# A corner table of two pixels a row, and the first chunk transposed by TensorE

## The chip, the cores and the metric

The kernel runs on one core of one Trainium2 chip. The metric is the device time of one execution in microseconds (us), as the median of the runs shown. The engines are named as in the profile: PE (TensorE, matrix products; PEld its weight loads), DVE (VectorE), ACT (ScalarE), POOL (GpSimd) and SP (SyncE). SP, ACT and POOL also issue DMAs; their queues are written SPq, ACTq and POOLq.

## The reference

The input `x` has 4 images of 128 channels and 64 x 64 pixels, in float32. Two layers are computed.

Layer 0 is `x + deform_conv(group_norm(x))`. A 3 x 3 convolution of the normalized image gives, for each output pixel and each of 9 taps, an offset in y and x and a mask. Every tap is sampled bilinearly at its shifted place, with zero outside the image, and the samples are multiplied with the weights:

```python
v00 = gather(y0i, x0i); v01 = gather(y0i, x1i)
v10 = gather(y1i, x0i); v11 = gather(y1i, x1i)
samples = v00*(1-wy)*(1-wx) + v01*(1-wy)*wx + v10*wy*(1-wx) + v11*wy*wx
out = jnp.einsum('bckhw,ock->bohw', samples * mask, w_flat) + bias
```

Layer 1 treats the 4096 pixels of an image as tokens of 128 features. It adds an attention block (16 heads of 8 dimensions, queries, keys and values all being one cosine feature map of the tokens, softmax over all 4096 keys, then a small feed-forward) and a layer of 8 experts of which the best two are mixed.

## The kernel before

An image is worked on in 8 chunks of 512 pixels. `prepare(b)` makes an image ready for attention, the main loop runs attention, and `finish` takes a finished chunk through the rest of layer 1. `prepare` and `finish` are generators that say before each piece what it needs of PE and DVE. A planner (`Beside`), which keeps its own clock from estimated costs, places their pieces beside the attention steps while the program is built. The result is a fixed order of instructions on every engine; each engine works through its own in order. Before the first chunk of image 0 is ready, only `prepare(0)` runs.

**`prepare(b)`** loads the image into `xc` (L766), normalizes it (L456), and builds a *corner table* in DRAM (`corner_table`). Before, a row of the table holds four pixels, the corners of one bilinear cell, 4 x 128 floats or 2 KB; there are 67 x 67 rows (`TW` = 67), two tables, used in turn. Each chunk of 1024 pixels is transposed by PE to tokens (`tok_ps`, L464), copied by DVE to `tok` (L467), and written to the table by DMAs (L476). Every pixel is a corner of four cells, so it is written four times: 8 DMAs of 256 KB for 1024 pixels (two row parities by four corners), each in pieces of 512 bytes, 32 DMAs an image. For image 0 they are shared evenly between SP and ACT, for the others all are on SP. `tok` shares its 3 buffers (tag `v`) with the gathered samples, so the fourth chunk waits until the first has been written. The rim of the table is zeroed by `borders` (L304, L305): for table 0 on ACT at the start, for table 1 on SP when image 1 begins. The constants are loaded on ACT after the borders.

**`offsets`** multiplies the image with the offset weights (`om_ps`, L507) in two halves, turns the result (`oc_ps`, L519) and computes on DVE the table index `idx` (L551) and the four bilinear weights `wt` (L557, L559), which include the mask `mk`. For the mask ACT computes an exponential (L529).

**`deform`** goes through the image in 96 units. A unit is 128 pixels and 3 taps. POOL gathers for each tap 128 table rows with one indirect DMA (L575), two units ahead of their use. DVE multiplies with the weights (L589) and adds the four corners (L591, L592). The samples then stand with pixels on partitions and the convolution needs channels there. So DVE transposes 32 x 32 blocks (L599, three a unit); after four units the result `tr` goes to a DRAM buffer `smd` in 4 DMAs on SP (L612) and comes back in 4 DMAs as `sT` with the blocks in place (L643). Twelve units, three such trips, make a chunk.

**`convolved`** multiplies `sT` with the 9 weight taps (`conv_ps`, issued through a helper, L273), adds bias and the input `xr` (L666), turns the result (`x_ps`, L673), and goes on to `features`: layer norm, the cosine features, and their parking in DRAM as `kTd`, `qTd` and `fqd`. Attention loads keys (`kT`, L1133), values (`qf`, L1135) and queries (`qT`, L1143) on SP from there.

**Attention** computes scores `sc` (L1155), exponentials on ACT (L1164) and sums `acc` (L1172). For image 0 it starts on the first chunk while the others are still prepared. Partial sums of such runs are parked in DRAM (`part`, L1031), loaded again as `cu` (L1344) and added (L1376); a run that needs no earlier sum is copied (L1374). In the later images exponentials are also reused transposed: parked as `etd` (L1056) and loaded as `et` (L1090, used at L1108), again on SP. All these loads and stores stand on SP in one order with the table writes.

Of the kernel before, what the change touches and what calls it, by code (L numbers as in the profile page):

```python
# [30 lines left out]
KK = 9  # L31
# [165 lines left out]
def need(pe=0.0, dve=0.0, lat=0.0, hold=False, after=0.0):  # L197

    return pe, dve, lat, hold, after
# [11 lines left out]
def tr(n):  # L213

    return 0.13 + 0.115 * n
# [3 lines left out]
def kernel(  # L219
# [74 lines left out]


    NTAB = 2
    tabs = [dram.tile([TW * TW, 4 * C], F32, name=f"tab{i}") for i in range(NTAB)]
    def borders(tab, queue):
        zero = work.tile([P, 4, 4, P], F32, tag="st", name="zero", bufs=NST)
        zero = zero.rearrange("p r h x -> p r (h x)")[:TW, :2]  # L300
        nc.gpsimd.memset(zero, 0.0)
        tv = tab.rearrange("(y x) c -> y x c", x=TW)
        for s in (0, TW - 2):
            queue.dma_start(out=tv[s : s + 2].rearrange("y x c -> x y c"), in_=zero)  # L304
            queue.dma_start(out=tv[2 : TW - 2, s : s + 2, :], in_=zero[: TW - 4])  # L305
# [143 lines left out]
    def corner_table(b, xc, mg, rs, tab):  # L449


        tv = tab.rearrange("(y x) (k c) -> y x k c", x=TW, c=C)
        for ch in range(NBLK // 8):
            yield need(dve=ve(1024), lat=0.3)
            part = xc[:, 1024 * ch : 1024 * (ch + 1)]
            nc.vector.tensor_scalar(part, part, mg, rs, ALU.subtract, ALU.mult)  # L456
            tok = work.tile([P, 3, 4 * C], F32, tag="v", name=f"tok{b}_{ch}", bufs=NV)
            tok = tok.rearrange("p k (q c) -> p (k q) c", c=C)[:, :8]
            for i in range(0, 8, 4):
                yield need(pe=tr(4), dve=ve(512), lat=FREE)  # L460
                pt = misc(f"tok_ps{b}_{ch}_{i}")
                for n in range(4):
                    j = 8 * ch + i + n
                    nc.tensor.transpose(  # L464
                        pt[:, C * n : C * (n + 1)], xc[:, P * j : P * (j + 1)], ident
                    )
                nc.vector.tensor_copy(  # L467
                    tok[:, i : i + 4, :], pt.rearrange("p (i c) -> p i c", c=C)
                )
            def put(ch=ch, tok=tok):  # L470
                for par in range(2):
                    for k in range(4):
                        y0 = 16 * ch + par + 2 - k // 2
                        x0 = 2 - k % 2
                        queue = nc.scalar if b == 0 and k % 2 else nc.sync
                        queue.dma_start(  # L476
                            out=tv[y0 : y0 + 15 : 2, x0 : x0 + WW, k].rearrange("y x c -> x y c"),
                            in_=tok[WW * par : WW * (par + 1)],
                        )

            beside.later(beside.dve, put)

    def offsets(b, xn, idx, wt):
# [3 lines left out]
        for half in range(2):  # L487
# [55 lines left out]
            def of_axis(t, a):  # L543
                return t.rearrange("p j (k a) -> p j k a", a=2)[:, :, :, a]
# [10 lines left out]
            for dy in range(2):  # L555
                yield need(dve=ve(144, 3), lat=0.2)
                nc.vector.tensor_tensor(ix, of_axis(p if dy else up, 0), mk, ALU.mult)  # L557
                for dx in range(2):
                    nc.vector.tensor_tensor(  # L559
                        wt[:, blk, :, 2 * dy + dx], ix, of_axis(p if dx else up, 1), ALU.mult  # L560
                    )

    def deform(b, tab, idx, wt):
# [19 lines left out]
        for n, (ch, kg, j) in enumerate(units):  # L583
            progress[b] = 0.1 + 0.9 * n / len(units)
            v, landed = ahead.pop(0)
            v4 = v.rearrange("p k (q c) -> p (k q) c", c=C)
            w12 = wt[:, j, 3 * kg : 3 * kg + 3, :].rearrange("p k q -> p (k q)")
            yield need(dve=ve(1536), after=landed)
            nc.vector.tensor_tensor(v4, v4, w12[:, :, None].to_broadcast([P, 12, C]), ALU.mult)  # L589
            yield need(dve=ve(768) + ve(384))  # L590
            nc.vector.tensor_tensor(v[:, :, : 2 * C], v[:, :, : 2 * C], v[:, :, 2 * C :], ALU.add)  # L591
            nc.vector.tensor_tensor(v[:, :, :C], v[:, :, :C], v[:, :, C : 2 * C], ALU.add)  # L592

            yield need(dve=ve(384))
            if j % 4 == 0:
                beside.flush(sent)
                tr9 = work.tile([P, 4, 4, 4, 32], F32, tag="st", name=f"tr{b}_{ch}_{kg}", bufs=NST)
            for k in range(3):
                nc.vector.transpose(  # L599
                    out=tr9[:, k, :, j % 4, :],  # L600
                    in_=v[:, k, :C].rearrange("p (c i) -> p c i", i=32),
                )
            if n + AHEAD < len(units):
                beside.later(beside.dve, lambda u=units[n + AHEAD]: ahead.append(gather(*u)))
            if j % 4 < 3:
                continue
            while kg == 0 and len(featuring) > 1:
                yield need(lat=1.0)

            def put(ch=ch, kg=kg, tr9=tr9):  # L610
                for o in range(4):
                    nc.sync.dma_start(  # L612
                        out=smd[ch % 2][:, 3 * kg : 3 * kg + 3, :, o].rearrange(
                            "i k c n -> i (k c) n"
                        ),
                        in_=tr9[32 * o : 32 * (o + 1), :3].rearrange("p k c j t -> p (k c) (j t)"),
                    )
# [12 lines left out]
        while featuring:  # L630
            yield need(lat=1.0)

    def convolved(b, ch):

        xr = work.tile([P, CH], F32, tag="p2", name=f"xr{b}_{ch}", bufs=NP2)
        nc.sync.dma_start(out=xr, in_=xf[b, :, CH * ch : CH * (ch + 1)])
        yield need(lat=2.5)

        sT = big.tile([P, KK, CH], F32, tag="xs", name=f"sT{b}_{ch}")

        def get(kg):
            for c in range(4):
# [2 lines left out]
                    in_=smd[ch % 2][:, 3 * kg : 3 * kg + 3, c].rearrange("i k o n -> i k (o n)"),  # L645
                )

        get(0)
        yield need(lat=6.0)
        get(1)  # L650
        yield need(lat=4.0)
        for k in range(KK):
            if k == 2:
                get(2)
            for hf in range(2):
                last = k == KK - 1 and hf == 1
# [6 lines left out]
                )  # L663
        for o in range(4):
            of_block = xr.rearrange("p (j o t) -> p j o t", o=4, t=32)[:, :, o]
            nc.vector.scalar_tensor_tensor(  # L666
                of_block, po[:, P * o : P * (o + 1)].rearrange("p (j t) -> p j t", t=32), bconv_sb,
                of_block, ALU.add, ALU.add,
            )
# [786 lines left out]
```

## Time and profile before

| | |
|---|---|
| median of 3 runs | 7870.18 us (7869.32 to 7878.19) |
| the profiled execution | 7908.98 us, span 7907.1 us |
| PE busy | 7194.3 us, 91% of the span |
| ACT busy | 6874.6 us, 87% |
| DVE busy | 4487.9 us, 57% |
| POOL busy | 1644.6 us, 21% |
| chain that ended last | PE 78%, DMA 8%, DVE 3%, SPq 3% |
| gathers (L575) | 1152, mean 1254 ns on POOL |
| table writes (L476) | 112 on SP, 16 on ACT |

The page gives one execution. Its span runs from the first to the last instruction; 1.9 us lie around it. Busy shares are averages over stages that have different limits, so the stages have to be looked at one by one: the page cuts the span in 40 slices, and the trace can be asked for the busy time of any stretch, for the instructions in order of time, and for what ended each engine's idle time.

### The profile page before, as it was taken

Reading aid. Unit: us, or ns where it says so; the run is one execution under the profiler, and the core shown is the slowest. Engines: PE = TensorE matmul, PEld = TensorE weight load, DVE = VectorE, ACT = ScalarE, POOL = GpSimd, SP = SyncE. Lnnn points to the kernel's source line nnn. Section 1 sums busy time; section 2 is a strip of 40 time slices with the busy share of each in tenths; the row PEclk is TensorE's granted clock in tenths of the full one; section 3 lists DMA queues with packets and bytes.
Section 4 is the critical chain, followed back from the end, with each engine's and each line's share of the span. In section 5 each row is a group of like instructions: output and inputs, shape, how many; then the busy total and the mean of one; then the engine's idle time right before and its main releaser. Section 6 shows DMA issues by size and latency. Waiting matters only on the chain.

```text
span 7907.1 us, 182019 instructions
## 1 busy us (share of the span) xinstructions
PE 7194.3 (91%) x73664; PEld 2524.1 (32%) x73664; DVE 4487.9 (57%) x9024; ACT 6874.6 (87%) x7441; POOL 1644.6 (21%) x1326
## 2 busy tenths in 40 slices
PE   2378979999998999999999989989999999999997
PEld 1122222333333333333333333333333333333333
DVE  5666436666453667777554567766444554445434
ACT  0267978988998988989999988888999999999995
POOL 4544114343100332332000133432000000000000
PEclk6688988999999999999999999999999999999998
DMA  6776558888666878898666788988655577877762
GB/s 180 215 214 208 158 150 251 272 260 269 194 190 181 254 228 254 261 293 266 189 187 180 211 278 270 286 282 276 188 175 168 157 234 238 256 240 247 241 212 81
DMA packets 968439, 1757.98 MB, mean 222 GB/s; under 512 B 170864, under 2 KB 436088, under 8 KB 916908
## 3 DMA queue, kind: packets, MB, share of 16 engines
q1 hardware_dynamic: 862590, 1436.61, 60.1%
q0 software_dynamic: 92160, 302.06, 11.9%
q8 instruction: 578, 9.47, 0.5%
q10 hardware_dynamic: 12846, 7.67, 0.4%
q14 instruction: 265, 2.17, 0.1%
HBM read 1063.83 MB, written 682.13 MB: 221 GB/s over the span
## 4 chain that ended last, share of the span: by engine, by line
PE 78%; DMA 8%; DVE 3%; SPq 3%; issue 3%; ACT 3%; POOL 1%; another core or an unknown queue 0%; ACTq 0%; DVEq 0%; POOLq 0%
PE acc L1172 38%; PE sc L1155 23%; PE acc L1108 5%; PE e_ps L273 3%; PE conv_ps L273 3%; ACT e L1164 3%; PE f_ps L273 2%; DMA sT<-smd 2%; DMA et<-etd 1%; DMA kT<-kTd 1%; DMA etd<-st 1%; SPq L476 1%; PE om_ps L507 1%; DMA v<-tab,idx 1%; DVE v L589 1%
## 5 line engine op out<-in xcount | busy, mean ns | idle before, releaser
L1164 ACT ACTIVATE e<-sc 128x1024 f32<-128x1024 f32 x7400 | 6871.5, 1065 | 863.7 <-PE sc L1155 584.6
L1172 PE MATMUL acc<-e,qf 128*32 128x512 f32 x29600 | 3982.3, 608 | 46.1 <-DVE cu L1376 32.9
L1155 PE MATMUL sc<-qT,kT 32*128 32x512 f32 x14800 | 2404.0, 502 | 317.8 <-ACT e L1164 148.2
L1155 PEld LDWEIGHTS sc<-qT,kT 32*128 32x128 f32 x14800 | 960.2, 184 | 3745.1 <-ACT e L1164 3089.6
L575 POOL DMA_INDIRECT v<-tab,idx x1152 | 1444.7, 1254 | 1880.2 <-DVE tr L599 1158.3
L1046 DVE STREAM_TRANSPOSE st<-e 128x1024 f32<-128x1024 f32 x792 | 937.8, 1222 | 833.1 <-ACT e L1164 640.7
L1172 PEld LDWEIGHTS acc<-e,qf 128*32 128x32 f32 x29600 | 804.0, 110 | 614.4 <-issue 339.8
L375 POOL TENSOR_TENSOR r<-ln_t,expo 128x4 f32<-128x4 f32 x96 | 112.3, 1170 | 3151.2 <-DVE ln_t L373 3113.4
L589 DVE TENSOR_TENSOR v<-v,wt 128x1536 f32<-128x1536 f32 x384 | 665.9, 1734 | 103.6 <-DMA v<-tab,idx 78.5
L1108 PE MATMUL acc<-et,qf 128*32 128x128 f32 x12672 | 528.7, 283 | 55.5 <-DMA et<-etd 47.5
L273 PE MATMUL conv_ps<-sT,wconv_sb 128*32 128x256 f32 x4608 | 380.7, 407 | 125.0 <-DMA sT<-smd 121.9
L970 DVE TENSOR_TENSOR eo<-e_ps,gt 128x512 f32<-128x512 f32 x256 | 175.0, 685 | 548.7 <-PE e_ps L273 538.3
L1108 PEld LDWEIGHTS acc<-et,qf 128*32 128x32 f32 x12672 | 305.7, 110 | 259.3 <-issue 191.9
L591 DVE TENSOR_TENSOR v<-v 128x768 f32<-128x768 f32 x384 | 367.3, 957 | 10.7
L1374 DVE COPY cu<-acc 128x512 f32<-128x512 f32 x128 | 88.5, 691 | 442.0 <-PE acc L1172 392.6
L599 DVE STREAM_TRANSPOSE tr<-v 128x128 f32<-128x128 f32 x1152 | 266.0, 282 | 39.0 <-DMA etd<-st 21.1
L592 DVE TENSOR_TENSOR v<-v 128x384 f32<-128x384 f32 x384 | 215.4, 561 | 13.3
L273 PEld LDWEIGHTS conv_ps<-sT,wconv_sb 128*32 128x32 f32 x4608 | 96.9, 110 | 274.6 <-issue 255.1
L375 POOL TENSOR_TENSOR rstd<-lt_t,expo 128x4 f32<-128x4 f32 x32 | 54.3, 1696 | 554.8 <-DVE lt_t L373 554.8
L273 PE MATMUL f_ps<-w_sb,h 128*32 128x128 f32 x4096 | 165.4, 281 | 0.0
L855 DVE TENSOR_SCALAR h<-h_ps,b_sb 128x512 f32<-128x512 f32 x128 | 94.8, 743 | 102.3 <-PE h_ps L853 96.0
L1376 DVE TENSOR_TENSOR cu<-cu,acc 128x512 f32<-128x512 f32 x38 | 26.1, 686 | 207.1 <-PE acc L1172 118.9
(219 smaller groups left out, 3008.8 us busy)
## 6 DMA issues: line engine op xcount, KB each, us to landing
etd<-st SPq DMA_DIRECT2D x1584, 256.0 KB
et<-etd SPq DMA_DIRECT2D x396, 1024.0 KB
kT<-kTd SPq DMA_DIRECT2D x400, 256.0 KB
smd<-tr SPq DMA_DIRECT2D x384, 192.0 KB
sT<-smd SPq DMA_DIRECT2D x384, 192.0 KB
qf<-fqd SPq DMA_DIRECT2D x400, 144.0 KB
qT<-qTd SPq DMA_DIRECT2D x166, 256.0 KB
atd<-cu SPq DMA_DIRECT2D x128, 256.0 KB
```

What stands on the lines that cost most here:

```text
L273: nc.tensor.matmul(dst[c : c + 32], lhsT=lhsT[:, c : c + 32], rhs=rhs, start=start, stop=stop)
L575: nc.gpsimd.indirect_dma_start(out=v[:, k, :], out_offset=None, in_=tab, in_offset=bass.IndirectOffsetOnAxis(ap=idx[:, j, kk : kk + 1], ax ...
L589: nc.vector.tensor_tensor(v4, v4, w12[:, :, None].to_broadcast([P, 12, C]), ALU.mult)
L591: nc.vector.tensor_tensor(v[:, :, : 2 * C], v[:, :, : 2 * C], v[:, :, 2 * C :], ALU.add)
L592: nc.vector.tensor_tensor(v[:, :, :C], v[:, :, :C], v[:, :, C : 2 * C], ALU.add)
L599: nc.vector.transpose(out=tr9[:, k, :, j % 4, :], in_=v[:, k, :C].rearrange("p (c i) -> p c i", i=32),)
L970: nc.vector.tensor_tensor(ws[hf], pe.rearrange("p (e c) -> p e c", c=C), gt[:, i, 4 * hf : 4 * (hf + 1), None].to_broadcast([P, 4, C]), AL ...
L1046: nc.vector.transpose(out=st[:, :, 2 * pr : 2 * pr + 2, :].rearrange("p o h (q j) -> p o (h q) j", j=32), in_=es[pr].rearrange("p h (q o i ...
L1108: nc.tensor.matmul(acc[32 * h : 32 * (h + 1), P * kt : P * (kt + 1)], lhsT=qf[:, t, QW * h : QW * h + 32], rhs=e[:, :, h, 32 * t : 32 * (t ...
L1155: nc.tensor.matmul(ps[i // 2][:, i % 2, :], lhsT=kT[h : h + 32, P * (t % 4) : P * (t % 4 + 1)], rhs=qT[h : h + 32, :], start=True, stop=True,)
L1164: nc.scalar.activation(e, ps[pr], AF.Exp, scale=1.0 / math.sqrt(HD))
L1172: nc.tensor.matmul(acc[32 * h : 32 * (h + 1), :], lhsT=qf[:, t % 4, QW * h : QW * h + 32], rhs=es[h // 2][:, h % 2, :], start=(t == ts[0]) ...
```

## The change

A table row now holds two pixels, the upper and the lower corner at one x, 2 x 128 floats or 1 KB. A gather still takes 2 KB from the row of its index, which is that row and the next, the corners at x + 1. One more row at the end of the table, zeroed by its own small DMA, keeps the last gather inside. A pixel is written twice instead of four times: 16 DMAs an image. For image 0 the row parity chooses the queue, ACT writing the odd rows of the first three chunks and SP all others, including both parities of the fourth. The borders keep their number of DMAs and halve their bytes. The weights `wt` change their order with the corners.

For the first chunk of image 0 the three tap blocks of a unit are transposed by PE into a PSUM bank and copied by DVE into `sT_first`; the trip through `smd` is left out. The pixels of that chunk stand in their natural order, so `convolved` takes `in_order` and loads nothing but `xr`. All other chunks go through `smd` as before. The planner is told of the new needs, and so it also places pieces of the first image's later chunks differently: for instance PE's convolution of the second chunk now begins in the fourth attention run and not in the second. From the end of that stretch on, PE's instructions stand in the same order as before.

```diff
-    tabs = [dram.tile([TW * TW, 4 * C], F32, name=f"tab{i}") for i in range(NTAB)]
+    tabs = [dram.tile([TW * TW + 1, 2 * C], F32, name=f"tab{i}") for i in range(NTAB)]
     def borders(tab, queue):
         zero = work.tile([P, 4, 4, P], F32, tag="st", name="zero", bufs=NST)
-        zero = zero.rearrange("p r h x -> p r (h x)")[:TW, :2]
+        zero = zero.rearrange("p r h x -> p r (h x)")[:TW, :2, : 2 * C]
         nc.gpsimd.memset(zero, 0.0)
-        tv = tab.rearrange("(y x) c -> y x c", x=TW)
+        tv = tab[: TW * TW].rearrange("(y x) c -> y x c", x=TW)
+        queue.dma_start(out=tab[TW * TW :], in_=zero[:1, 0])
...
             def put(ch=ch, tok=tok):
                 for par in range(2):
-                    for k in range(4):
-                        y0 = 16 * ch + par + 2 - k // 2
-                        x0 = 2 - k % 2
-                        queue = nc.scalar if b == 0 and k % 2 else nc.sync
+                    for k in range(2):
+                        y0 = 16 * ch + par + 2 - k
+                        queue = nc.scalar if b == 0 and par == 1 and ch < 3 else nc.sync
                         queue.dma_start(
-                            out=tv[y0 : y0 + 15 : 2, x0 : x0 + WW, k].rearrange("y x c -> x y c"),
+                            out=tv[y0 : y0 + 15 : 2, 2 : 2 + WW, k].rearrange("y x c -> x y c"),
                             in_=tok[WW * par : WW * (par + 1)],
                         )
...
-                        wt[:, blk, :, 2 * dy + dx], ix, of_axis(p if dx else up, 1), ALU.mult
+                        wt[:, blk, :, 2 * dx + dy], ix, of_axis(p if dx else up, 1), ALU.mult
...
+            if (b, ch) == (0, 0):
+
+                if (kg, j) == (0, 0):
+                    sT = big.tile([P, KK, CH], F32, tag="xs", name="sT_first")
+                yield need(pe=tr(3), dve=ve(384))
+                pt = misc(f"sT_ps{j}_{kg}")
+                for k in range(3):
+                    nc.tensor.transpose(pt[:, P * k : P * (k + 1)], v[:, k, :C], ident)
+                nc.vector.tensor_copy(
+                    sT[:, 3 * kg : 3 * kg + 3, P * j : P * (j + 1)],
+                    pt[:, : 3 * P].rearrange("p (k c) -> p k c", c=P),
+                )
+                if n + AHEAD < len(units):
+                    beside.later(beside.dve, lambda u=units[n + AHEAD]: ahead.append(gather(*u)))
+                if (kg, j) == (2, 3):
+                    featuring.append(True)
+                    beside.add("prepare", convolved(b, ch, sT), 0.5, True)
+                continue
...
-    def convolved(b, ch):
+    def convolved(b, ch, sT=None):
...
+        in_order = sT is not None
+        if not in_order:
+            yield need(lat=2.5)
+
+            sT = big.tile([P, KK, CH], F32, tag="xs", name=f"sT{b}_{ch}")
...
+        if not in_order:
+            get(0)
+            yield need(lat=6.0)
+            get(1)
+            yield need(lat=4.0)
         for k in range(KK):
-            if k == 2:
+            if k == 2 and not in_order:
                 get(2)
...
+            if in_order:
+                of_block = xr[:, P * o : P * (o + 1)].rearrange("p (j t) -> p j t", t=32)
```

More of the change, by code (lines that the diff above doesn't have):

```diff
@@ L449, in corner_table @@
     def corner_table(b, xc, mg, rs, tab):
-        tv = tab.rearrange("(y x) (k c) -> y x k c", x=TW, c=C)
+        tv = tab[: TW * TW].rearrange("(y x) (k c) -> y x k c", x=TW, c=C)
         for ch in range(NBLK // 8):
@@ L631, in deform @@
             yield need(lat=1.0)
-    def convolved(b, ch):
+    def convolved(b, ch, sT=None):
         xr = work.tile([P, CH], F32, tag="p2", name=f"xr{b}_{ch}", bufs=NP2)
         nc.sync.dma_start(out=xr, in_=xf[b, :, CH * ch : CH * (ch + 1)])
-        yield need(lat=2.5)
-        sT = big.tile([P, KK, CH], F32, tag="xs", name=f"sT{b}_{ch}")
+        in_order = sT is not None
+        if not in_order:
+            yield need(lat=2.5)
+            sT = big.tile([P, KK, CH], F32, tag="xs", name=f"sT{b}_{ch}")
         def get(kg):
@@ L646, in get @@
                 )
[L648 to L651, printed above, removed]
+        if not in_order:
[3 more added lines that the diff above has]
+            yield need(lat=4.0)
         for k in range(KK):
-            if k == 2:
+            if k == 2 and not in_order:
                 get(2)
```

## The prediction

> **What bounds the kernel now.** Part 2 of the page, slice by slice, says that TensorE (PE) is full from about 800 us on, and nearly idle before 250. So I read three stretches where PE waits: the start, the change of image near 1000 us, and two short ones later. First the busy time by stage (columns: stretch, length, then PE, weight loads, DVE, ACT, POOL, granted clock, DMA share, GB/s), then the instructions in order of time (start, duration, engine or queue, line; in brackets the idle time before it and what ended it).
>
> ```profile
> 50.00:100.00 50.00, 12.56 (x152) 6.95 (x152) 23.20 (x61) 1.95 (x3) 8.98 (x9) 0.60 0.72 178
> 100.00:150.00 50.00, 0.00 (x0) 0.00 (x0) 40.32 (x62) 0.00 (x0) 39.20 (x27) 0.50 0.59 168
> 200.00:250.00 50.00, 4.78 (x20) 2.27 (x24) 41.01 (x81) 3.79 (x5) 32.31 (x24) 0.50 0.66 208
> ```
>
> ```profile
> 13.00 9.00 ACTq L305 DMA_DIRECT2D tab<-zero  x1
> 34.23 10.28 PE L507 MATMUL om_ps<-xc,wom_sb 128*32 128x256 f32 x144 [5.01 <-DMA wom_sb<-in_wom_dram]
> 34.56 35.24 SPq L476 DMA_DIRECT2D tab<-tok  x16
> 49.25 28.60 ACTq L476 DMA_DIRECT2D tab<-tok  x16
> 61.66 1.29 DVE L467 COPY tok<-tok_ps 128x512 f32<-128x512 f32 x2 [34.53 <-DMA tab<-tok]
> 77.88 1.28 ACT L529 ACT_TABLE_LOAD   x1 [77.88 <-DMA tab<-tok]
> 79.54 0.23 DVE L546 TENSOR_SCALAR mk<-mk 128x144 f32<-128x144 f32 x1 [11.11 <-ACT mk L529]
> 98.53 1.76 DVE L589 TENSOR_TENSOR v<-v,wt 128x1536 f32<-128x1536 f32 x1 [0.23 <-issue]
> 115.54 43.78 SPq L612 DMA_DIRECT2D smd<-tr  x12
> 174.06 5.24 PE L273 MATMUL conv_ps<-sT,wconv_sb 128*32 128x256 f32 x48 [88.72 <-DMA sT<-smd]
> 192.31 1.12 DVE L666 SCALAR_TENSOR_TENSOR xr<-conv_ps,bconv_sb,xr 128x128 f32<-128x128 f32 x4 [4.71 <-remote]
> 245.38 1.22 PE L1155 MATMUL sc<-qT,kT 32*128 32x512 f32 x6 [27.09 <-DMA kT<-kTd]
> ```
>
> The start is one chain: zero borders, constants behind them, table writes, offsets (DVE at 61.66 waits for a token buffer until chunk 0's table writes land; `mk` waits because ScalarE's own queue is still issuing table writes), 12 gather units from 98.5, the trip through DRAM (last unit's multiply 152.43, conv 174.06), features, first scores at 245.38. At the next image the same writes stand on SP ahead of loads that PE needs:
>
> ```profile
> 980.99 8.89 SPq L305 DMA_DIRECT2D tab<-zero  x1
> 990.55 11.13 SPq L305 DMA_DIRECT2D tab<-zero  x1
> 1013.40 0.80 PE L1155 MATMUL sc<-qT,kT 32*128 32x512 f32 x4 [22.86 <-DMA kT<-kTd]
> 1037.86 31.60 SPq L476 DMA_DIRECT2D tab<-tok  x24
> 1074.54 0.69 DVE L1376 TENSOR_TENSOR cu<-cu,acc 128x512 f32<-128x512 f32 x1 [31.30 <-DMA cu<-part]
> 1075.29 1.94 PE L1172 MATMUL acc<-e,qf 128*32 128x512 f32 x8 [16.89 <-DVE cu L1376]
> 2509.77 1.08 PE L1108 MATMUL acc<-et,qf 128*32 128x128 f32 x16 [11.15 <-DMA et<-etd]
> ```
>
> [...] In the DMA view of 0 to 35 us (40 slices of 0.87 us) the rate lies at 26 GB/s[...] for most of 10 to 34 us:
>
> ```profile
> GB/s 0 5 146 212 407 385 391 418 354 325 159 37 26 26 105 185 49 26 26 26 26 26 26 28 23 96 152 199 52 26 26 26 23 26 26 26 28 21 196 358
> ```
>  [...] A gather issue takes 0.95 us beside nothing and 1.85 when it starts under L589[...].
>
> **The change, part by part.**
>
> *Borders, half the bytes.* 134 pieces of 2 KB at 26 GB/s are 79 ns each, 10.6 us a DMA. A table write has 32 pieces of 512 B an engine and takes 31.60/24 = 1.32 us, 41 ns a piece. A straight line puts a 1 KB piece at 54 ns: 7.2 us. Two of them save 7 us; by bytes alone it would be 10.6. I take 8: drained at 26 instead of 34. The extra row is one 1 KB piece, 0.5 us of issue.
>
> *Image 0's table: 32 writes become 16, ten on SP and six on ACT.* From the first load after the borders (32.4) to ACT's first table write (49.25) is 17 us; then from 25 to 42. In the built program each DMA of SP and ACT waits for the one eight places before it, so at most eight are under way, and ACT's two writes of chunk 0 land some 9 us later (the last before took 8.97): the token copy comes at 51 instead of 61.66, 11 earlier. Chunk 3's writes pass from ACT to SP, so ACT is free by about 51 and `mk` (its input `om` at 55) no longer waits: 11.11 falls to 0. Late next is the second offsets product on PE: in before 75.1 − 61.66 = 13.5 after the copy, against 21.8 for L514 behind `mk`. That is 8 more; together **19**, first unit at 79.5. SP's ten writes end near 60; two units of gathers (6 × 1.27) follow and land by 72, still covered.
>
> *Chunk 0's transposes.* Out: 36 stream transposes (0.28 each, 10 us of DVE) and 24 DMAs of 192 KB on SP (12 L612, 12 L643). In: 36 PE transposes (L673: four in 1.08, so 0.8 for a unit) and 12 copies (128x432 took 0.61, so 0.55). DVE now waits for PE in each unit, with the next unit's multiply queued behind it, and POOL's next gather waits for PE to have read the buffer; PE has nothing else there (0.00 busy in 100 to 150). With 0.95 from DVE's last add to the end of PE's transposes (oc_ps: 1.2 for four), a unit's DVE loop goes from 4.1 to 3.4 + 0.95 + 0.55 = 4.9 us. Units now come every 53.9/11 = 4.9, because three gather issues on POOL and their landing set it; POOL gets the buffer 0.2 later. I charge 2 us over the 12 (bounds: −3, as 24 DMAs leave, to +8). The twelfth multiply stands at 79.5 + 56 = 135.5 and its copy ends at 140.4. Conv starts there, without the put, the load and its 2.6 of stalls: from conv's start to L666 was 18.2, now 15.6, so L666 at 156 against 192.31, **36** earlier. First scores follow by as much; `kT_0` now stands ahead of chunk 1's last puts on SP.
>
> *What of 36 lasts.* Later chunks go on through DRAM and share DVE and POOL with the features. Their units start 17 earlier at least. But PE's new order puts conv_1 behind three runs, where before PE stood in front of kT and sT_1 (27.09, 8.99) with DVE waiting behind it (8.71 and 12.69 at L1374). PE is nearly full from 700 to 980, and after conv_7 its order is the same line for line, so what is gained by then stays. I take **33**; bounds 10 (deform's pace eats it) and 45.
>
> *Image 1.* The two stalls, 20 us,[...] shrink by a third to a half: kT lands 13 earlier of 22.86. The 24 writes become 12, 15.8 us less on SP, so `cu` is there before PE comes: 16.89 goes. Sum 30 less 1 for the extra row and a load: **29** (18 to 36).
>
> *Images 2 and 3.* 16 writes fewer on SP, some 1.25 us each, ahead of `et` loads whose waits there are 3.34 + 11.15 and 4.30 + 4.47: **11** of 23 (0 to 18), as etd's own puts stay.
>
> At nothing: the four weights in another order (same instructions); the output blocks in order (same four L666); gathers (same index, same 2 KB).
>
> Sum 33 + 29 + 11 = **73 us** of the profiled run's 7908.98 (span 7907.1 and 1.9 around). The median shown is 7870.18, 0.5% lower; 73 scales to as good as 73, so **7797**. The bounds added are 28 and 99: 7771 to 7842 for this case.
>
> **Rivals.**
> - *A, as summed*, 0.72.
> - *B, the opening's gain is swallowed.* POOL is at 39 of 50 us in 100 to 150; if the gathers alone set every later chunk, and the features only move, chunk 0 is early and waits for chunk 1. Left are 29 + 11, 7830. For it: DVE waits for gathers at 334 and 350. Against: the long DVE waits there are for PE. 0.18.
> - *C, no change:* the writes are held by the eight places and their latency, not by bytes; everything slides together. Within 15 us of 7870. Against: 26 GB/s flat. 0.03.
> - *D, slower:* a gather that spans two rows is split. L575 then issues twice the pieces: 288 gathers of image 0 at +0.95 (its shortest) are +274 on the loop that POOL sets, less 73: 8070. It decides from 73/288 = 0.25 us a gather. For it: the row is now 1 KB and the tile's piece 2 KB. Against: the two rows adjoin, and the destination is one run. 0.07, of which 0.01 ends near no change.
>
> A measurement of this kernel can tell about 0.2% (16 us) from no change. From the cases: faster 0.90, same 0.04, slower 0.06. The range, 7765 to 7850, is A's own with B's lower gains.
>
> **What would show it.** Right: L467 after its wait near 51, no ACT wait before L546, first L589 near 80, L666 near 156, first scores near 210; the kT wait near 10 and no `cu` wait at the next image; PE's idle lines at 2477 to 2510 and 4342 to 4383 shorter. Wrong: L575's mean above 1.5 us (D), units of chunk 0 over 5.5 us apart, or conv_5 to conv_7 at the old times (B).

## The result, and the profile after

The changed kernel takes 7742.14 us, median of 4 runs (7735.5 to 7757.48), against 7869.75 us for the kernel before on the same chip (4 runs, 7863.6 to 7878.19): a ratio of **0.9838 (0.9825 to 0.9850)**, 128 us faster. Run twice more it gave 0.9841 (0.9827 to 0.9854) and 0.9845 (0.9825 to 0.9865). The direction was forecast, the size was not: 73 us were predicted, and the result lies outside the range.

The profiled execution has a span of 7735.7 us. First the timeline of its opening (start, duration, engine or queue, line, tiles; in brackets the idle time before it and what ended it). Some lines have other numbers than before: L306 was L305, L468 was L467, L689 was L666, L1178 was L1155; L600 and L601 are new.

```profile
10.13 6.25 ACTq L306 DMA_DIRECT2D tab<-zero  x1
16.48 0.66 ACTq L312 DMA_DIRECT2D wom_sb<-in_wom_dram  x1
25.58 23.64 SPq L476 DMA_DIRECT2D tab<-tok  x10
36.22 8.16 ACTq L476 DMA_DIRECT2D tab<-tok  x6
42.58 1.29 DVE L468 COPY tok<-tok_ps 128x512 f32<-128x512 f32 x2 [14.00 <-DMA tab<-tok]
44.41 1.28 ACT L529 ACT_TABLE_LOAD   x1 [44.41 <-DMA tab<-tok]
49.20 0.23 DVE L546 TENSOR_SCALAR mk<-mk 128x144 f32<-128x144 f32 x1
69.81 1.76 DVE L589 TENSOR_TENSOR v<-v,wt 128x1536 f32<-128x1536 f32 x1
73.26 0.87 PE L600 MATMUL sT_ps<-ident,v 128*128 128x128 f32 x3 [16.27 <-DVE v L592]
74.17 0.56 DVE L601 COPY sT_first<-sT_ps 128x384 f32<-128x384 f32 x1 [1.01 <-PE sT_ps L600]
74.64 1.75 DVE L589 TENSOR_TENSOR v<-v,wt 128x1536 f32<-128x1536 f32 x1
127.10 9.40 PE L273 MATMUL conv_ps<-sT_first,wconv_sb 128*32 128x256 f32 x144
139.59 1.09 DVE L689 SCALAR_TENSOR_TENSOR xr<-conv_ps,bconv_sb,xr 128x128 f32<-128x128 f32 x4
190.07 1.22 PE L1178 MATMUL sc<-qT,kT 32*128 32x512 f32 x6 [24.58 <-DMA kT<-kTd]
```

The chain has the same links as before, each one sooner. The token copy comes at 42.6 instead of 61.7, ACT's table load at 44.4 instead of 77.9, so `mk` has no wait; the first unit's multiply stands at 69.8 instead of 98.5. A unit of chunk 0 takes 4.83 us (69.81 to 74.64), with DVE waiting 1.01 for PE's transposes. The first scores come 55 us earlier. They still wait 24.6 for `kT`, which is the trip of chunk 0's features through DRAM.

At the next image the same lines read:

```profile
911.72 5.75 SPq L306 DMA_DIRECT2D tab<-zero  x1
918.23 5.20 SPq L306 DMA_DIRECT2D tab<-zero  x1
931.68 0.80 PE L1178 MATMUL sc<-qT,kT 32*128 32x512 f32 x4 [9.92 <-DMA kT<-kTd]
942.75 4.36 SPq L476 DMA_DIRECT2D tab<-tok  x4
950.11 14.69 SPq L476 DMA_DIRECT2D tab<-tok  x12
975.08 0.69 DVE L1399 TENSOR_TENSOR cu<-cu,acc 128x512 f32<-128x512 f32 x1 [14.20 <-PE acc L1195]
```

The border stalls of SP fell from 8.89 and 11.13 to 5.75 and 5.20, PE's wait for `kT` from 22.86 to 9.92, and the wait for `cu` (16.89) is gone: DVE's addition of `cu` (L1399, L1376 before) now waits for PE and no longer for the load. 12 table writes stand together on SP there, not 24.

**The two traces at hand don't compare one to one.** The profiled execution of before took 7908.98, 39 us above the median, so the traces differ by 171 us and the medians by 128. A second trace of before was therefore taken first.

### The profile page after: what moved, and what is told of

It reads as the page before. It is cut to its first block, busy times and chain, and to the rows that moved or that the text cites. A ratio compares the mean times of both kernels' runs of the same rounds, so it can differ in the third digit from the quotient of the medians.

```text
span 7735.7 us, 181988 instructions
## 1 busy us (share of the span) xinstructions
PE 7156.1 (93%) x73700; PEld 2517.5 (33%) x73700; DVE 4484.8 (58%) x9000; ACT 6871.2 (89%) x7441; POOL 1648.3 (21%) x1326
## 4 chain that ended last, share of the span: by engine, by line
PE 81%; DMA 7%; DVE 4%; issue 2%; ACT 2%; SPq 2%; another core or an unknown queue 0%; POOL 0%; ACTq 0%; POOLq 0%; DVEq 0%
PE acc L1195 39%; PE sc L1178 24%; PE acc L1131 5%; PE e_ps L273 4%; PE conv_ps L273 3%; ACT e L1187 2%; PE f_ps L273 2%; DMA sT<-smd 1%; DMA et<-etd 1%; PE om_ps L507 1%; DMA etd<-st 1%; DVE v L589 1%; DMA kT<-kTd 1%; DMA qT<-qTd 1%; PE ao_ps L273 1%
## 5 line engine op out<-in xcount | busy, mean ns | idle before, releaser
L1187 ACT ACTIVATE e<-sc 128x1024 f32<-128x1024 f32 x7400 | 6868.1, 1068 | 724.7 <-PE sc L1178 470.2
L1178 PE MATMUL sc<-qT,kT 32*128 32x512 f32 x14800 | 2390.7, 500 | 292.4 <-ACT e L1187 153.6
L1178 PEld LDWEIGHTS sc<-qT,kT 32*128 32x128 f32 x14800 | 956.3, 183 | 3697.6 <-ACT e L1187 3078.1
L575 POOL DMA_INDIRECT v<-tab,idx x1152 | 1444.7, 1254 | 1754.5 <-DVE tr L617 1108.1
L1131 PE MATMUL acc<-et,qf 128*32 128x128 f32 x12672 | 521.3, 281 | 36.4 <-DMA et<-etd 30.5
L591 DVE TENSOR_TENSOR v<-v 128x768 f32<-128x768 f32 x384 | 367.9, 958 | 10.5
L592 DVE TENSOR_TENSOR v<-v 128x384 f32<-128x384 f32 x384 | 215.5, 561 | 13.3
L754 POOL COPY fx<-rn 128x512 f32<-128x512 f32 x32 | 28.9, 904 | 528.9 <-DVE rn L753 328.1
```

The source lines that it names most:

```text
L575: nc.gpsimd.indirect_dma_start(out=v[:, k, :], out_offset=None, in_=tab, in_offset=bass.IndirectOffsetOnAxis(ap=idx[:, j, kk : kk + 1], ax ...
L1131: nc.tensor.matmul(acc[32 * h : 32 * (h + 1), P * kt : P * (kt + 1)], lhsT=qf[:, t, QW * h : QW * h + 32], rhs=e[:, :, h, 32 * t : 32 * (t ...
L1178: nc.tensor.matmul(ps[i // 2][:, i % 2, :], lhsT=kT[h : h + 32, P * (t % 4) : P * (t % 4 + 1)], rhs=qT[h : h + 32, :], start=True, stop=True,)
L1187: nc.scalar.activation(e, ps[pr], AF.Exp, scale=1.0 / math.sqrt(HD))
```

## The experiments

All kernels issue the same 7400 exponentials on ACT (L1164 before, L1187 after) in one order, so the start of the k-th (k from 0) tells how far one execution is ahead of another at that point of the work. In the table, times of the second trace of before and of the changed kernel, and differences to that trace of before, in us. The rows are the first scores, a point near the end of image 0's preparation, a point after image 1's start, two around image 2's start, two around image 3's, and the end.

| k | before, second trace (e1) | changed | changed − before | table only (e2) | PE transposes only (e3) | changed, old order (e4) |
|---|---|---|---|---|---|---|
| 0 | 243.0 | 190.9 | −52.1 | −25.7 | −24.9 | −36.8 |
| 480 | 873.4 | 825.2 | −48.2 | −10.0 | −20.0 | −26.8 |
| 720 | 1146.7 | 1064.9 | −81.8 | −42.0 | −20.8 | −56.9 |
| 1920 | 2367.9 | 2284.8 | −83.2 | −44.0 | −11.5 | −48.7 |
| 2160 | 2623.7 | 2519.2 | −104.5 | −65.6 | −13.3 | −70.2 |
| 3840 | 4291.7 | 4187.0 | −104.7 | −55.5 | −17.6 | −72.8 |
| 4080 | 4542.1 | 4423.2 | −118.9 | −69.3 | −15.5 | −86.1 |
| 7399 | 7773.3 | 7651.1 | −122.2 | −69.1 | −22.6 | −91.6 |

These are single executions, and runs of one kernel on one chip differ by 10 to 55 us; a few us in the table mean nothing.

**e1, before again.** No edit.

> The kernel before, unchanged, for a second trace of it. Between the two traces at hand (7907.1 and 7735.7 us of span) lie 171 us, between the medians 128. If the first trace was simply a slow execution (my account), this one has a span near 7868, the same stalls in the first 1100 us within a few us, and a difference to the changed kernel's trace that still stands near 100 at image 1's first convolution and grows by only 25 to 35 afterwards. If the growth from 104 at image 1 to 171 at the end is a gain of the change (rival), the same drift shows here too and the span comes out above 7900.

Measured: 7860.02, span 7858.1. The first trace of before was a long execution: it fell behind the second by 20 us in the opening (k = 480) and by 48 up to the end, with stalls of much the same size. The second trace is the one to subtract from: opening 48, image 1 33.6, image 2's start 21.3, image 3's start 14.2, together 117 of 122. So the opening ends at 48, not at the 69 that the first trace suggested, and about 40, not the 67 or so of the first trace, come after image 1's start.

**e2, the table only.**

```diff
-            if (b, ch) == (0, 0):
+            if (b, ch) == (-1, 0):
```

> Table of two pixels a row, queues and weights as changed; chunk 0's samples go through DRAM again, and PE's order is the one of before. The first unit's multiply should stand near 70, as in the changed kernel. My account: the table brings its lead of 29 to the first unit, some of which lasts (20 to 29), all of image 1's 33 and what the later images gain (20 to 30): 73 to 92 of the 128, so 7780 to 7797, first scores near 216. Rival 1 (chunk 0's transposes and the order that follows from them make most of the opening's gain): only 33 and the later images' share stay, 7805 to 7820. Rival 2 (a lead of the table is eaten by the trips through DRAM, as the prediction's case B had it for later chunks): the same 7805 to 7820, but with first scores at 216 and chunk 7 at the old time.

Measured: 7782.06 against 7860.82, ratio 0.9879 (0.9853 to 0.9905). The sum fits my account, its parts don't. The table's lead of 26 at the first scores shrinks to 10 by k = 480, as rival 2 said; image 1 gives 32 and the two later starts 21.6 and 13.8. That is as good as all that the changed kernel gains at these three starts; it doesn't need the PE transposes.

**e3, the PE transposes only.** Before, with the block for chunk 0 and `in_order`; table, weights and queues of before.

```diff
-                    for k in range(2):
-                        y0 = 16 * ch + par + 2 - k
-                        queue = nc.scalar if b == 0 and par == 1 and ch < 3 else nc.sync
+                    for k in range(4):
+                        y0 = 16 * ch + par + 2 - k // 2
+                        x0 = 2 - k % 2
+                        queue = nc.scalar if b == 0 and k % 2 else nc.sync
```

> The table of four pixels a row with all its writes and queues as before; only chunk 0's samples are transposed by PE, and PE's order is the one of the changed kernel. First unit near 98.5. My account: the trip through DRAM is worth 55.3 - 28.7 = 26.6 at the first scores, so they stand near 219, and of that 20 to 40 lasts to chunk 7 (units of chunks 1 to 7 are not sooner than before, so at most a little over 27): 7830 to 7850, with image 1's waits of 22.9 and 16.9 as before. Rival (the later order, conv_1 after three runs, is itself worth the growth of the lead from 42 at chunk 1 to 69 at chunk 7): 50 or more, 7820 or below.

Measured: 7845.35, ratio 0.9972 (0.9956 to 0.9989). As my account had it: 25 us at the first scores, 20 at k = 480, and nothing at the later images' starts. The rival's 50 is excluded. The order of PE, DVE and SP in this run is that of the changed kernel, so its 20 hold the worth of that order too.

**e4 and e6, the changed kernel with the old order.** PE's order of the opening is brought back by telling the planner that chunk 0 comes later. DVE and SP get their order of before with it:

```diff
             sT = big.tile([P, KK, CH], F32, tag="xs", name=f"sT{b}_{ch}")
+        else:
+            yield need(lat=15.0)
```

> The changed kernel, but the planner is told that chunk 0's convolution comes 15 us later than in the changed kernel, by which PE's order of the opening becomes that of before but for chunk 0's transposes (16 lines of difference against 218). My account (the leads make the gain, not the order): within 10 us of the changed kernel's 7742, and chunk 7 within 10 us of its time there (900). Rival (conv_1 behind three runs gives the growth of the lead from 42 to 69): 20 to 30 us slower, 7762 to 7772, with PE waiting for sT_1 and conv_1 with DVE behind it as in before (27, 9).

> The changed kernel with PE's order of before in the opening, again, since three rounds left 0.9867 (0.9838 to 0.9896) against 0.9838. Its trace reached chunk 7's features at 921.9 instead of 900.5. My account, changed by that trace: the order is worth 20 to 25 us of the 128, so this one is 18 to 28 us slower than the changed kernel beside it. Rival (the leads alone; the 21 us were one execution's): within 8 us of it.

Measured: 7771.11, ratio 0.9867 (0.9838 to 0.9896), and again 7633.00 beside 7611.86 for the changed kernel, 0.9868 (0.9852 to 0.9883) against 0.9841. Both times it is slower, by 21 us where both ran side by side. My first account, that the leads alone make the gain, fell: of the opening's 48, some 20 go with the new order. Here are two of PE's waits from 180 to 880 us (us in total, times, longest), first in e6, then in e5, the changed kernel run beside it:

```profile
PE conv_ps L273 <- DMA sT<-smd: 31.1, 3, 20.5
PE sc L1180 <- DMA qT<-qTd: 29.3, 3, 14.1
```

```profile
PE conv_ps L273 <- DMA sT<-smd: 13.7, 2, 7.9
PE sc L1178 <- DMA qT<-qTd: 17.4, 3, 13.6
```

With the old order PE reaches the convolutions and the queries before their data have come back from DRAM; it has 29 us more of such waits. Other waits differ by as much the other way: `kT` with 73.1 in the new order, against 30.5 in the old and another 29.0 before the first scores that the trace puts down to `smd`, and `cu` with 26.3 against 8.5. So these sums don't show where the 21 come from. Nor is it PE's order alone. In e6 chunk 0's own features come later, since PE waits 13.27 us for DVE's `xr` (2.85 in e5), and `kT` of chunk 0 stands behind four `smd` puts on SP. e6 is 18 us behind e5 at the first scores, 8 at k = 240 and 21 at k = 480. What is shown is the worth of the planner's new placement as a whole.

For the lead at k = 480 this gives 10 for the table alone, 27 with the PE transposes in the old order, and 48 with the new order. The parts don't add up singly: beside e3, which has the transposes and the new order, the table is worth 28. Why it keeps so much more of its lead there is not shown.

> The changed kernel once more, beside the next three. Expected as measured: 0.984 of the kernel before (some 126 us), features of chunk 7 near 900, image 1's kT wait near 10.

Measured: 7611.86 against 7737.44, ratio 0.9841 (0.9827 to 0.9854), kT wait 10.86. The chip on which e5 to e8 ran takes 1.7% less for either kernel than the one of the result, so their exponentials are compared only with each other.

**e7, the table writes of images 1 to 3 issued twice**, the second time into a table that nobody reads:

```diff
                             in_=tok[WW * par : WW * (par + 1)],
                         )
+                        if b > 0:
+                            queue.dma_start(
+                                out=tw[y0 : y0 + 15 : 2, 2 : 2 + WW, k].rearrange("y x c -> x y c"),
+                                in_=tok[WW * par : WW * (par + 1)],
+                            )
```

> The changed kernel, in which for images 1 to 3 every table write is issued a second time, into a table that nobody reads: SP issues as many table writes of as many bytes as before, the borders stay halved. My account (image 1's cu wait and the later images' et waits are SP's places and time taken by these writes): the cu wait of 17 comes back at image 1's start, the et waits go from 31 to some 52 us, together 38 slower, 7780; the kT wait stays near 10. Rival (the later gain comes from elsewhere: the work of the later images simply meets PE at another phase): within 10 us of the changed kernel.

Measured: 7667.06, ratio 0.9915 (0.9902 to 0.9929): 55 us slower than the changed kernel. The waits come back where before had them. PE in e7, at the starts of images 1, 2 and 3:

```profile
908.49 0.80 PE L1185 MATMUL sc<-qT,kT 32*128 32x512 f32 x4 [10.88 <-DMA kT<-kTd]
968.80 1.93 PE L1202 MATMUL acc<-e,qf 128*32 128x512 f32 x8 [16.67 <-DVE cu L1406]
2374.32 1.08 PE L1138 MATMUL acc<-et,qf 128*32 128x128 f32 x16 [11.02 <-DMA et<-etd]
4189.59 1.08 PE L1138 MATMUL acc<-et,qf 128*32 128x128 f32 x16 [6.33 <-DMA et<-etd]
```

The second trace of before at the latter two:

```profile
2482.66 1.08 PE L1108 MATMUL acc<-et,qf 128*32 128x128 f32 x16 [12.50 <-DMA et<-etd]
4343.13 1.08 PE L1108 MATMUL acc<-et,qf 128*32 128x128 f32 x16 [4.87 <-DMA et<-etd]
```

Against e5, the k-th exponentials of e7 are 3 sooner at k = 480, then 15 later at 720, 21 at 1920, 41 at 2160, 38 at 3840 and 51 at 4080: steps of 18, 20 and 13 at the three starts, against 33.6, 21.3 and 14.2 gained by the change. So the later images' gain comes from the table writes on SP, and so does half of image 1's; the rival is out. (The run doubles the number and the bytes of these writes together, so which of the two counts is not shown.) The queue itself shows the writes at work. SP in the second trace of before, ahead of the 12.50 wait, and in the changed kernel at the same place:

```profile
2444.74 12.45 SPq L476 DMA_DIRECT2D tab<-tok  x8
2457.29 1.36 SPq L1019 DMA_DIRECT2D atd<-cu  x1
2458.70 1.36 SPq L1143 DMA_DIRECT2D qT<-qTd  x1
2460.16 9.58 SPq L476 DMA_DIRECT2D tab<-tok  x8
2469.84 4.90 SPq L1056 DMA_DIRECT2D etd<-st  x4
2474.84 1.35 SPq L1090 DMA_DIRECT2D et<-etd  x2
```

```profile
2350.18 7.36 SPq L476 DMA_DIRECT2D tab<-tok  x4
2357.66 0.94 SPq L1042 DMA_DIRECT2D atd<-cu  x1
2358.93 1.15 SPq L1166 DMA_DIRECT2D qT<-qTd  x1
2360.19 4.01 SPq L476 DMA_DIRECT2D tab<-tok  x4
2364.81 4.10 SPq L1079 DMA_DIRECT2D etd<-st  x4
2369.01 1.79 SPq L1113 DMA_DIRECT2D et<-etd  x2
2381.69 0.64 PE L1131 MATMUL acc<-et,qf 128*32 128x128 f32 x16
```

From the first line to the `et` loads it is 30.1 us before and 18.8 after, as 16 writes became 8. PE's wait of 12.50 for `et` is gone; the last line, its product with the same tile, has no wait. Before, the load was issued 4.7 us after PE was ready for it (at 2482.66 − 12.50 = 2470.16). In the changed kernel it is issued 12.7 us ahead of its use. That is 17.4 us sooner against PE: 11.3 from the writes shown, the rest because SP comes to this stretch sooner against PE.

The waits are not the whole of these steps. For the stretches between the same exponentials the trace gives PE's busy time (the same work), what is left of the stretch as its idle time, and the mean granted clock:

| k | idle, e1 → changed | busy | clock | idle, e5 → e7 | busy | clock |
|---|---|---|---|---|---|---|
| 480 to 720 | 42.5 → 12.9 | 230.8 → 226.8 | 0.91 → 0.97 | 11.8 → 28.5 | 224.4 → 225.6 | 0.97 → 0.94 |
| 1920 to 2160 | 21.6 → 5.7 | 234.2 → 228.7 | 0.95 → 0.99 | 0.4 → 15.7 | 223.3 → 228.2 | 1.00 → 0.97 |
| 3840 to 4080 | 15.4 → 7.3 | 235.0 → 228.9 | 0.96 → 0.99 | 0.0 → 10.2 | 222.4 → 224.9 | 1.00 → 0.99 |

In all six pairs of this table the execution with more idle time has the longer busy time too, at the lower granted clock. Behind the 12.50 wait this can be seen directly (columns as in the prediction: stretch, length, PE, weight loads, DVE, ACT, POOL, granted clock, DMA share, GB/s), first in the second trace of before, then at the same product in the changed kernel:

```profile
2482.70:2487.00 4.30, 4.30 (x48) 2.06 (x52) 0.00 (x0) 0.73 (x1) 0.00 (x0) 0.50 1.02 395
2381.00:2386.00 5.00, 5.00 (x84) 2.35 (x84) 2.37 (x2) 5.00 (x7) 0.00 (x0) 1.00 0.09 27
```

PE is busy throughout in both, at clock 0.50 and at 1.00, and the product that had waited took 1.08 us, the other 0.64. e7 adds nothing but table writes, and in it both the waits and the slower work come back. At images 2 and 3 together the change took away 24 us of idle time and some 12 of slower work.

**e8, table 1's borders issued twice.**

```diff
             queue.dma_start(out=tv[2 : TW - 2, s : s + 2, :], in_=zero[: TW - 4])
+            if queue is nc.sync:
+                tw = twin[: TW * TW].rearrange("(y x) c -> y x c", x=TW)
+                queue.dma_start(out=tw[s : s + 2].rearrange("y x c -> x y c"), in_=zero)
+                queue.dma_start(out=tw[2 : TW - 2, s : s + 2, :], in_=zero[: TW - 4])
```

> The changed kernel, in which only the four border writes of table 1 (image 1) are issued a second time into an unread table[...]. My account (the first part of image 1's gain is these bytes): the kT wait goes from 10 to some 20, 10 to 13 us slower, 7752 to 7755. Rival (kT is late for its own place on SP or because PE comes to it earlier or later, not for the borders): no change over 3 us in the kT wait.

Measured: 7619.36, 7.5 above the changed kernel; the intervals overlap (0.9852, 0.9837 to 0.9867), so the time alone doesn't prove it. The wait does:

```profile
918.88 0.80 PE L1183 MATMUL sc<-qT,kT 32*128 32x512 f32 x4 [22.75 <-DMA kT<-kTd]
```

10.86 became 22.75, the size of before. The exponentials at k = 720 are 8 later, less than the wait, since this execution had come there 3.5 to 5 earlier. So the other half of image 1's gain is the borders. The run doubles their number as well as their bytes, and the kernel before had only the bytes. The spread borders below, with number and bytes unchanged, take this wait away as well.

**e9 and e13, the 67-row borders over all partitions.**

```diff
-            queue.dma_start(out=tv[s : s + 2].rearrange("y x c -> x y c"), in_=zero)
+            queue.dma_start(
+                out=tab[TW * s : TW * (s + 2)].rearrange("y c -> (y c)").rearrange("(p n) -> p n", p=P),
+                in_=rim,
+            )
```

> The changed kernel, with the two 67-row border writes of a table written as 128 pieces of 1072 bytes over 128 partitions[...] (same bytes, same places). My account: [...]both the start and image 1's kT stand behind them. Then the borders drain some 8 us sooner, the wait of the token copy falls from 14 to 6 to 10, first scores 4 to 8 earlier, the kT wait of image 1 falls from 10.9 to under 4: 8 to 14 us faster than the changed kernel, 0.9825 of before. Rival (ACT's 20 us of constants set the start, and kT waits for SP's places): under 4 us in all, the kT wait over 8.

> The changed kernel with the 67-row border writes spread over 128 partitions, again. In its first trace the first scores came 7 us sooner, the kT wait of 10.9 was gone and image 1 stood 15 to 18 sooner, of which 2 were left at 3600 us. Account A (these leads are worth little at the end, the later images give them back): within 6 us of the changed kernel. Account B (that trace met a slower stretch; the leads last): 12 to 20 us faster.

> The changed kernel beside the next three, so that they can be compared on one chip in one session. Expected: 0.984 of the kernel before, as twice.

Measured: e9 7735.21, 0.9849 (0.9828 to 0.9869); e13 7764.08 beside e12, the changed kernel, at 7771.64: 0.9836 (0.9816 to 0.9856) against 0.9845 (0.9825 to 0.9865). What stands behind the borders comes sooner, as expected: ACT's first table write is issued at 28.4 in e13 instead of 35.8 in e12, the token copy stands at 34.7 instead of 42.2, and image 1's kT wait is 0.99 and not 11.04. So the same bytes as 128 pieces over 128 partitions don't hold these up as the two 67-row writes did; why is not shown. Yet no gain could be measured. The first unit comes only 3 to 5 sooner. In e9's trace a lead of 13 at k = 720 over the changed kernel's first trace, on another chip, was gone by the end; in e13's it was kept against an execution of e12 that was itself 17 us above its median. Whether a few us remain is left open.

**e10 and e14, table 0's borders issued twice**, as in e8, at the start:

```diff
-            if queue is nc.sync:
+            if queue is nc.scalar:
```

> The changed kernel, in which the four border writes of table 0 at the start are issued a second time, into an unread table[...]. My account: wom goes from 16.5 to 22, ACT's first table write from 36 to 44, the token copy from 42.6 to 51, first unit near 79, that is the half bytes are 8 to 11 of the 29 us by which the first unit came sooner; some 6 to 9 of it last, 0.985 of before. Rival (the table writes themselves, fewer and in another share, make the 29): first unit within 4 us of 70.

> The changed kernel with table 0's border writes issued twice, again. The first trace was 9.5 us later at the first scores, 12 at chunk 7 and 25 at the end. Account A (a lead of the start is kept up to chunk 7 and then blurred by the later images, either way): 5 to 25 us slower than the changed kernel. Account B (a lead of the start is kept one for one): 10 to 14 slower, with the same shift from chunk 7 to the end.

Measured: first unit at 80.84 in e10, 11 us later than 69.81; k = 0 is 9.8 later than in the changed kernel's trace. That is my account's 8 to 11, though by way of larger delays in between: `wom` at 28.9 and the token copy at 54.9, since ACT now issues eight border writes in a row. Totals: 7762.36 (0.9878, 0.9858 to 0.9898) and 7794.73 (0.9870, 0.9848 to 0.9892), the latter 23 above e12. By the traces e10 is 12 later at k = 480 and 25 at the end. That would be more than one for one, but the interval holds the 12 as well. In e14's trace the delay against e12's is 12 at the first scores and 5 at k = 480, and e12's was a long execution. How much of a delay at the start arrives at the end is not settled.

**e11, chunk 3's odd rows back on ACT.**

```diff
-                        queue = nc.scalar if b == 0 and par == 1 and ch < 3 else nc.sync
+                        queue = nc.scalar if b == 0 and par == 1 else nc.sync
```

> The changed kernel, but chunk 3's four odd-row writes of image 0 are on ACT again instead of SP. My prediction's step: ACT then waits for the fourth chunk's token copy with its exponential behind it, so the table load goes from 44.4 to some 50 or later, mk waits 4 to 9 us, the first unit comes as much later, and 3 to 8 last. Rival (in the changed kernel ACT is free long before mk's input is there, and SP's queue is the longer one): first unit within 2 us of 70, or earlier, as SP has four writes fewer; no change within the noise.

Measured: 7751.83, 0.9866 (0.9845 to 0.9887), not separable from the changed kernel. The table load moves from 44.4 to 47.1, and `mk` at 48.85 has still no wait: the rival was right.

```profile
36.15 10.94 ACTq L476 DMA_DIRECT2D tab<-tok  x8
47.12 1.28 ACT L529 ACT_TABLE_LOAD   x1 [47.12 <-DVE fl L535]
48.85 0.23 DVE L546 TENSOR_SCALAR mk<-mk 128x144 f32<-128x144 f32 x1
```

So ACT is free in time even with chunk 3's odd rows: the move wasn't needed.

**e15, spread borders, and chunk 0's writes all on SP.**

```diff
-                        queue = nc.scalar if b == 0 and par == 1 and ch < 3 else nc.sync
+                        queue = nc.scalar if b == 0 and par == 1 and 0 < ch < 3 else nc.sync
```

> As the spread borders, and image 0's first chunk of table writes all on SP instead of half of them on ACT behind its 20 us of constants. The token copy waits for the first chunk's writes to land: from 35 it should come to 30 to 32, as SP's first four writes are issued by 25 and land some 6 later; first scores another 2 to 4 sooner. At the end: under 4 us against the spread borders, not measurable, if the account A of that run is right.

Measured: 7766.22, 0.9839 (0.9820 to 0.9857), not separable from e12 or e13. The token copy indeed no longer waits for table writes. What stands behind it does; e13 first, then e15:

```profile
34.70 1.29 DVE L473 COPY tok<-tok_ps 128x512 f32<-128x512 f32 x2 [6.25 <-DMA tab<-tok]
40.15 0.75 DVE L519 TENSOR_SCALAR oc<-om_ps,bom_sb 128x512 f32<-128x512 f32 x1 [4.16 <-PE om_ps L512]
67.16 1.76 DVE L594 TENSOR_TENSOR v<-v,wt 128x1536 f32<-128x1536 f32 x1
```

```profile
30.13 9.74 PE L512 MATMUL om_ps<-xc,wom_sb 128*32 128x256 f32 x144
39.94 0.75 DVE L519 TENSOR_SCALAR oc<-om_ps,bom_sb 128x512 f32<-128x512 f32 x1 [9.01 <-PE om_ps L512]
67.06 1.76 DVE L594 TENSOR_TENSOR v<-v,wt 128x1536 f32<-128x1536 f32 x1
```

DVE's idle time merely moves to PE's offsets product, and the first unit stays at 67; the first scores come 0.9 sooner, where 2 to 4 were expected. In this version the first chunk's table writes have ceased to bound the start. No version measured here beats the changed kernel beyond its interval.

## Why the prediction was wrong

The mechanisms that it named were found, but two terms of its sum were too small: that of images 2 and 3 most of all, and what lasts of the opening. At images 2 and 3 it let a share of each wait stay and left out that PE ran slower behind a wait (at clock 0.50 behind the one of 12.50 us); in the opening it put no number on the planner's new order. By its steps:

- **Borders: the direction right, the price of a piece too high.** In the DMA views of 0 to 35 us (0.87 us a slice) the last stretch of 21 to 28 GB/s ahead of the constants ends with the 37th slice before (32.4 us) and with the 25th after (21.9): 10.5 sooner, 8 forecast. From the fifteenth to the nineteenth number after GB/s it is some 24 GB/s, 43 ns for 1 KB and not 54. The 54 was an estimate: one end of its line took the table writes as shared evenly by the 16 engines, and the DMA share during them was 0.87 (1037.86 to 1069.46 before); at the other end, from 16 to 22 us before, it was 0.07. The prediction took 34 for the end of the borders. That is where SP's first table write stands, 34.56 and now 25.58; the traces end its wait with small constants behind the borders. So 26 was met in part by luck, and the loads behind the borders started sooner than it assumed: `wconv` was issued at 21.6 and not at 25.

```profile
GB/s 0 0 149 156 412 392 388 423 284 78 207 331 171 35 21 25 25 23 25 117 106 114 23 25 23 61 232 343 102 63 313 139 229 200 242 196 171 147 339 341
```

- **Token copy and `mk`: undersized.** Forecast 51, first unit 79.5 (−19); measured 42.6 and 69.8 (−28.7). From `wconv` to ACT's first write it was 14.6, not 17, and the writes landed some 6 us after it, not 9. The mk wait fell to 0 as forecast, though e11 shows the move of chunk 3's writes wasn't needed for it.
- **Chunk 0's units: right.** 4.83 apart against 4.9; PE's detour of 1.01 (0.95 forecast). From the first unit to L689 it was 69.8 us, 76.5 forecast: conv to L689 took 12.5 instead of 15.6, and the 2 us charged didn't show. So the scores came 52 earlier (second trace of before), not 36.
- **What lasts of it: undersized.** Forecast 33, bounds 10 and 45; measured 48. The fear behind the lower bound was partly right. Alone, the table's lead fell from 26 to 10 (e2), as rival B has it. But the planner's new order is worth some 20 (e6): with it 48 of 52 last. The prediction had seen the new order and put no number on it.
- **Image 1: right.** 29 forecast, 33.6 measured: the `kT` wait went from 22.2 to 9.9 by the borders (e8), PE's wait for `cu` from 17.2 to 0.7 by the writes (e7). Some 4 of the 33.6 are PE's own work at a higher clock (0.97, not 0.91, from k = 480 to 720), which the prediction did not count.
- **Images 2 and 3: the term that failed most.** Forecast 11 of 23, since etd's own puts stay; measured 21.3 + 14.2, more than all of the 23. It was wrong twice. The puts stay, but they don't keep a share of the wait: with 8 of the 16 table writes gone, the `et` load was issued 17.4 us sooner against PE, and the wait of 12.50 went whole. In all some 24 us of waiting went. And a wait was counted at its length: some 12 us more are PE's own work, done at a higher clock with these waits gone (0.99, not 0.95 and 0.96, in the table's stretches). e7 brings both back, 33 us in sum.

With the measured values the sum is 48 + 33.6 + 35.5 = 117 of a trace difference of 122; the forecast had 33 + 29 + 11. The missing 44 are 15 in the opening, 4.6 at image 1 and 24.5 later. **D** is out: L575 has a mean of 1254 ns in both kernels, so a gather over two rows cost POOL no more. **C** is out as well: the kernel is 128 us faster.

Left open: why a lead or delay of the start or at image 1 arrives at the end sometimes whole (e6), sometimes not (e9), sometimes, as far as the medians tell, enlarged (e10, e14).

## What to carry to other kernels

When a queue holds loads that an engine needs behind bulk writes, price each wait on its own as a deadline: ask by how much the load comes sooner against the engine that needs it. If that is more than the wait (here 17.4 against 12.5 us), the whole wait goes, and no share of it stays for what is left in the queue. Then add what the engine loses behind the wait (here some 12 us of slower work on 24 us of waiting). A change that makes a planner place other work differently needs a number of its own for the new placement. And before differences of two traces are added up, compare each trace's own time with its median: here some 40 us of the apparent gain were one long execution.

## What the runs showed of the hardware that was not expected

- Behind a wait of 12.5 us PE was granted a clock of 0.50 for the next 4.3 us of unbroken work; without the wait, the same place in the work ran at 1.00. In the table's stretches at the starts of images 2 and 3 PE's own work took some 12 us more at the lower clock (0.95 and 0.96, not 0.99), on top of 24 us of waiting.
- The borders drained at 26 GB/s in pieces of 2 KB (16 to 22 us before, DMA share 0.07) and at some 24 in pieces of 1 KB (12.25 to 16.62 us in the changed kernel, 0.07). Here half the piece cost 2 of 26 GB/s.
- Chips differ: the kernel before took medians of 7870, 7737 and 7896 us on three of them, while the ratio of the changed kernel to it was 0.9838, 0.9841 and 0.9845.
